# Gates of six groups projected after the scan, in two-level block products, in a Mamba2 layer with LoRA experts on one core

## The chip, the core and the metric

The kernel runs on one core of a Trainium2 chip, in fp32 throughout. The core has a matmul engine (TensorE, "PE" in the profile), three engines for elementwise work (VectorE "DVE", ScalarE "ACT", GpSimd "POOL"), and a queue for transfers ("SP"). The metric is the time of one execution on the device in microseconds.

## The reference

A block of a network with 2048 tokens of 1024 channels. The input is normalised (layer norm without weights) and goes to two branches, whose sum is added to the input.

The first branch is a Mamba2 layer. `in_proj_w` projects to gate (4096 channels), x (4096), B and C (1024 each) and dt (64 heads). There are 8 groups; a group has 512 channels of the gate, 512 of x, 128 of B and 128 of C.

```python
gate = proj[..., :I]
hbc = proj[..., I:I + CONV_DIM]
...
xBC = jax.nn.silu(conv)                  # causal, 4 taps, over hbc
...
state = state * dA_t[..., None, None] + dtx_t[..., None] * B_t[:, :, None, :]
y_t = jnp.einsum('bhpn,bhn->bhp', state, C_t)
...
y = jnp.moveaxis(ys, 0, 1) + x * D[None, None, :, None]
yn = (yg * lax.rsqrt(var + EPS)).reshape(B, L, I) * norm_weight   # var per group
yn = yn * jax.nn.silu(gate)
out = jnp.einsum('bli,di->bld', yn, out_proj_w)
```

So the gate is needed only at the end: it multiplies the normalised output of the scan just before the output projection. The second branch is a linear layer of 1024 x 1024 with bias ("base") plus a mixture of rank-16 adapters, two of eight for each token.

## The kernel before

Channels lie on the partitions and tokens along the free axis. The sequence has two halves of 1024 tokens (`s` = 0, 1), each of two blocks of 512.

**Projections.** The big products save arithmetic by Strassen's scheme (Winograd's form). `pair` takes two tiles of 128 output channels over one half of the sequence: a matrix of 2 x 2 blocks times one of 2 x 2 blocks, in 7 block products instead of 8. A product is 4 matmuls of 128 x 128 weights with 512 tokens, accumulated in a bank of PSUM (`pa`, `px`, `py` of the pool `ps_proj`, four banks). The products come in the order 1, 6, 5, 2, 7, 3, 4; the banks are pa for 1 and 2, px for 6, 7 and 4, py for 5 and 3. In between, ScalarE copies (`s1`) and VectorE adds (L478, L482, L531) take the sums out, and each finished quarter is stored to memory (`stored`). The sums of weights (`s1` to `s4`) are made by GpSimd for the first half (L427) and kept in memory for the second.

`in_pairs` sets the order of the pairs: for each half and each group, three pairs of x, B and C and two pairs of the gate (whose quarters get the SiLU and go to `gate_d`), in all 40 per half; then four pairs of the base layer for each half, the second half first. The generator `stream` walks through this order one product at a time, and loads a pair's weights one pair ahead.

**The scan.** Behind the first five pairs runs the scan. `blocks` are 32 (half, group, block), each with four chunks of 128 tokens, so there are 128 slots. A slot mixes by hand, in program order, products of the stream (`products`) with the work of one chunk: `scan_b` of this chunk (ps_y, ps_e and ps_st on TensorE, then the output, and the state's update on GpSimd and VectorE) and `scan_a` of the next (on VectorE a scan of the decays `es`, and the mask `dab`; on TensorE the product `ps_cb` and the transposes of x, `ps_xt`, both in the bank "aux"; on ScalarE `xdt` and `xdd`). Around these lie the convolution of the next block (`conv`, in the second and third slot of a block), the norm and the multiplication with the gate for the block before (`norm_gate`, first slot), the squares (`norm_squares`, last slot), in the first half the layer norm of the second half (`ln_next`, `small`), and in the second half the sums of the output weights for the two-level scheme (`out_sums`, 16 sets on GpSimd, one per block). How many products each slot gets is set by `plan`:

```python
plan = [(0, 7 * PRE), (n_slots // 2 - NQ, 7 * (5 * G + 5)), (n_slots, total)]
```

With PRE = 5, G = 8 and 88 pairs in all this makes 280 products for the first 60 slots and 287 for the other 68. The last two pairs (POST = 2, 14 products) are kept for behind the scan.

**The output stage.** The output projection runs in four passes (second half of the sequence first) in the two-level scheme: 7 outer units of 7 inner products, each product 8 matmuls with 256 tokens (banks pa, px, py again). Its weights come from the sums in memory, its operands from `y_d`, and the additions to the result are on VectorE. The 14 products that were kept run while its first loads come in.

TensorE's instructions, GpSimd's sums and some of ScalarE's are kept in program order; the others may be placed by the compiler of the tile language by what they depend on. The functions that the change touches:

## Time and profile before

| what | value |
|---|---|
| median of 3 runs | 3439.4 us (3437.9 to 3439.51) |
| the profiled execution | 3437.5 us |
| its span on the core | 3435.7 us |
| mean granted clock of TensorE | 0.998 |
| busy: TensorE / VectorE / ScalarE / GpSimd | 3404.6 / 2410.5 / 1338.9 / 697.2 us |
| moved by DMA | 769.85 MB, mean 224 GB/s |

The profile is one execution. Every matmul in fp32 is two records in it. The duration of a record includes the end of its pipeline, which overlaps the next record, so the distance from start to start is the better price. In the order of time, `x8` is a merged run of eight records, and the bracket behind a row says how long the engine had been idle and what ended that. In the groups of instructions, the columns are line, engine and operation, output and inputs with their shapes, the count, then busy time and mean duration in ns, and last the idle time of the engine before them with what ended it. A line can be that of a helper: all matmuls are L79, and the sums on GpSimd L83. Windows give the busy time of each engine in a stretch of the span, with the number of instructions in parentheses, and then the clock, the share of DMA and GB/s.

### The profile page before, as it was taken

What the parts mean: (1) busy time and instruction counts of PE and PEld (TensorE: products, weight loads), DVE (VectorE), ACT (ScalarE), POOL (GpSimd) and SP (SyncE); (2) the same over time, 40 slices, a digit from 0 to 9 for tenths busy, and PEclk for the clock granted to TensorE, in tenths of its full rate; (3) what the DMA queues carried; (4) which work ended last, traced back from release to release, by engine and by line L of the source; (5) the groups of instructions that cost most, each with busy time, mean ns of one, the idle gap of its engine ahead of it and who ended that gap; (6) DMA issues with size and microseconds to landing.
All of it is one profiled execution on the core that took longest, in us unless ns stands there. A gap on an engine that the chain in (4) does not pass through costs nothing.

```text
span 3435.7 us, 38674 instructions
## 1 busy us (share of the span) xinstructions
PE 3404.6 (99%) x12820; PEld 1989.8 (58%) x12820; DVE 2410.5 (70%) x2733; ACT 1338.9 (39%) x3694; POOL 697.2 (20%) x443
## 2 busy tenths in 40 slices
PE   9999999999999999999999999999999999999999
PEld 7444544544545544544455454454454588888888
DVE  7547776877877867777777877777875466566665
ACT  2245454554555454545545455555453000000000
POOL 4123223222222211332222332222321000000000
PEclk9999999999999999999999999999999999999999
DMA  6546655655666676887778787877777777585654
GB/s 236 190 166 198 209 184 187 216 183 196 207 196 209 196 261 219 287 261 242 235 246 256 235 255 249 254 237 240 242 237 260 256 274 242 195 300 187 214 164 144
DMA packets 530327, 769.85 MB, mean 224 GB/s; under 512 B 35152, under 2 KB 264656, under 8 KB 527440
## 3 DMA queue, kind: packets, MB, share of 16 engines
q1 hardware_dynamic: 530128, 767.39, 68.7%
q8 instruction: 102, 1.67, 0.2%
q14 instruction: 97, 0.79, 0.1%
HBM read 516.64 MB, written 250.61 MB: 223 GB/s over the span
## 4 chain that ended last, share of the span: by engine, by line
PE 87%; DVE 8%; issue 2%; DMA 2%; ACT 2%; SPq 0%; DVEq 0%; ACTq 0%
PE ps_x_x L79 12%; PE ps_x_w L79 8%; PE ps_a_x L79 8%; PE ps_y_x L79 8%; PE ps_x_g L79 8%; PE ps_y_w L79 6%; PE ps_a_w L79 6%; PE ps_y_g L79 5%; PE ps_a_g L79 5%; PE ps_y L79 3%; PE ps_e L79 3%; PE ps_st L79 3%; PE ps_x_b L79 2%; DVE xg L646 2%; PE ps_a_b L79 2%
## 5 line engine op out<-in xcount | busy, mean ns | idle before, releaser
L83 POOL TENSOR_TENSOR state<-state,tot 128x512 f32<-128x512 f32 x112 | 150.2, 1341 | 1307.6 <-PE ps_e L79 1175.7
L688 DVE TENSOR_TENSOR_SCAN es<-dab,here 128x1024 f32<-128x1024 f32 x128 | 303.5, 2371 | 82.6 <-ACT xdd L728 81.3
L646 DVE SCALAR_TENSOR_TENSOR xg<-rawx,cw,xg 128x512 f32<-128x512 f32 x384 | 338.3, 929 | 16.8 <-ACT xg L640 15.9
L79 PE MATMUL ps_x_w<-t,w 128*128 128x256 f32 x1344 | 303.8, 379 | 0.0
L720 ACT ACTIVATE xdt<-ps_xt,dt 128x64 f32<-128x64 f32 x1024 | 223.0, 331 | 203.6 <-PE ps_xt L88 203.6
L79 PEld LDWEIGHTS ps_x_w<-t,w 128*128 128x128 f32 x1344 | 255.4, 190 | 41.5 <-issue 7.7
L705 ACT ACTIVATE ps_y<-xg,dsk 128x128 f32<-128x128 f32 x512 | 190.2, 371 | 222.5 <-DVE xg L770 192.9
L1345 ACT COPY s<-ps_a_w 128x512 f32<-128x512 f32 x28 | 16.4, 585 | 636.2 <-PE ps_a_w L79 555.6
L728 ACT ACTIVATE xdd<-xdt,es 128x64 f32<-128x64 f32 x1024 | 261.7, 387 | 0.0
L83 POOL TENSOR_TENSOR wo<-wo 128x512 f32<-128x512 f32 (+1 forms) x112 | 211.9, 1892 | 6.8
L709 DVE TENSOR_TENSOR dab<-es,cbm 128x1024 f32<-128x1024 f32 x128 | 177.6, 1388 | 39.3 <-ACT cbm L698 39.0
L79 PE MATMUL ps_a_w<-q,w 128*128 128x256 f32 x896 | 202.5, 379 | 0.0
L79 PEld LDWEIGHTS ps_a_w<-q,w 128*128 128x128 f32 x896 | 170.2, 190 | 23.6 <-issue 0.5
L79 PE MATMUL ps_x_x<-op_again,s_x 128*128 128x512 f32 x384 | 172.7, 592 | 0.0
L79 PE MATMUL ps_y_x<-op_again,s_x 128*128 128x512 f32 x384 | 172.7, 592 | 0.0
L79 PE MATMUL ps_a_x<-op_again,a_x 128*128 128x512 f32 x384 | 172.7, 592 | 0.0
L79 PEld LDWEIGHTS ps_y<-dab,xdt 128*64 128x64 f32 x2048 | 112.8, 137 | 102.9 <-issue 40.8
L79 PE MATMUL ps_x_x<-op,s_x 128*128 128x512 f32 x368 | 165.5, 592 | 0.0
L79 PE MATMUL ps_y_x<-op,s_x 128*128 128x512 f32 x368 | 165.5, 592 | 0.0
L79 PE MATMUL ps_a_x<-op,a_x 128*128 128x512 f32 x368 | 165.4, 592 | 0.0
L646 DVE SCALAR_TENSOR_TENSOR bc<-rawb,cw,bc 128x512 f32<-128x512 f32 x192 | 163.8, 885 | 1.9 <-ACT bc L640 1.3
L531 DVE TENSOR_TENSOR ev<-ps_x_x,s_x 128x512 f32<-128x512 f32 x94 | 64.4, 686 | 129.3 <-PE ps_x_x L79 124.2
(238 smaller groups left out, 6152.1 us busy)
## 6 DMA issues: line engine op xcount, KB each, us to landing
w<-w SPq DMA_DIRECT2D x196, 512.0 KB, 3.7
dab<-da_d SPq DMA_DIRECT2D x128, 512.0 KB, 5.4
raw<-ev SPq DMA_DIRECT2D x192, 256.0 KB, 3.3
a_x<-in_w_in_dram SPq DMA_DIRECT2D x168, 256.0 KB, 4.0
w<-wo SPq DMA_DIRECT2D x96, 448.0 KB, 4.3
ecp<-run_d SPq DMA_DIRECT2D x256, 128.0 KB, 4.0
gate<-ev SPq DMA_DIRECT2D x128, 256.0 KB, 3.6
sg<-gate SPq DMA_DIRECT2D x32, 1024.0 KB, 7.8
```

The lines of the kernel that those rows point to most:

```text
L79: tc.keep_in_program_order(nc.tensor.matmul(*args, **kw))
L83: ins = nc.gpsimd.tensor_tensor(*args)
L531: nc.vector.tensor_tensor(e, ps, add, alu)
L646: nc.vector.scalar_tensor_tensor(dst[:, i, :], raw[:, i, k : k + TB], cw[:, ti, k : k + 1], dst[:, i, :], ALU.mult, ALU.add,)
L688: nc.vector.tensor_tensor_scan(es.rearrange("p h t -> p (h t)"), dab.rearrange("p h t -> p (h t)"), here, 0.0, ALU.mult, ALU.add,)
L705: nc.scalar.activation(psy[:, j, :], xg[:, j, cs], AF.Copy, scale=dsk[:, at : at + 1])
L709: nc.vector.tensor_tensor(ms, es, cbm.unsqueeze(1).to_broadcast([P, HG, Q]), ALU.mult)
L720: ins = nc.scalar.activation(xdt[:, h, :], x_t[:, h, :], AF.Copy, scale=dt_of[s][:, half * NQ + c, at : at + 1],)
L728: ins = nc.scalar.activation(xdd[:, h, :], xdt[:, h, :], AF.Copy, scale=es[:, h, Q - 1 : Q])
L1345: nc.scalar.copy(s1, pa)
```

## The change

The gates of groups 0 to 5 (`2 * NO`, with NO = 3) leave the stream. It then has 28 pairs per half instead of 40, and `plan` spreads these over the same 128 slots; `products` takes `min(n - 3, 1)` where a slot has only three. In `norm_gate` these groups are normalised and stored without the gate.

Behind the scan and behind the last 14 products comes a new stage of 2 halves x 3 pairs of groups (`o`) x 7 outer units. A unit is 7 inner products of 4 matmuls with 256 tokens. Its left operands come from `w_in` or, for four of the seven units, from sums `s_d`, which `oct_sums` makes on GpSimd (for the first `o` in the last block of the scan, for the others in the stage), and GpSimd makes the second level of sums in `left_two`. The right operands' second level is made on VectorE (`right_two`) once per half. The results are gathered in SBUF (`acc_g`), get the SiLU on ScalarE, are multiplied on VectorE with the normalised y, which is loaded again from `y_d`, and stored in `yg_d` (`gated`). The output stage reads these groups from `yg_d`.

Further: of the 16 sets of output-weight sums 11 stay in the scan (two blocks of three) and 5 go to the second half of the new stage. The transposes of x take the bank "st" in place of "aux"; the sums of the layer norm, `ps_tot` and `ps_sm` take "aux". The output stage goes through the first half of the sequence first. The pool of the operands (`op`) is closed after the gate stage.

```diff
+NO = 3
...
-        ps = over_channels(of, "st", f"mean_{s}_{i}")
+        ps = over_channels(of, "aux", f"mean_{s}_{i}")
...
-                for q in range(2):
+                for q in range(2 if g >= 2 * NO else 0):
                     t = 4 * g + 2 * q
                     yield pair(
...
-        pst = ps_one.tile([P, 4, Q], F32, tag="aux", name=f"ps_xt_{n}")
+        pst = ps_one.tile([P, 4, Q], F32, tag="st", name=f"ps_xt_{n}")
...
-            nc.vector.tensor_tensor(two, two, sg_of[s, g, half][:, j : j + 2, :], ALU.mult)
+            if g >= 2 * NO:
+                nc.vector.tensor_tensor(two, two, sg_of[s, g, half][:, j : j + 2, :], ALU.mult)
             nc.sync.dma_start(y_d[g][:, j : j + 2, at : at + TB], two)
...
-    plan = [(0, 7 * PRE), (n_slots // 2 - NQ, 7 * (5 * G + 5)), (n_slots, total)]
+    plan = [(0, 7 * PRE), (n_slots // 2 - NQ, 7 * (N_S + 4)), (n_slots, total)]
...
-        if 0 <= b - 15 < 16:
-            left_sums = out_sums(wo, b - 15)
+        summing = 0 <= b - 15 < 16 and (b - 15) % 3 < 2
+        if summing:
+            left_sums = out_sums(wo, n_sums)
+            n_sums += 1
...
+    order = (1, 2, 6, 5, 7, 3, 4)
+    gate_units = [(s, o, i) for s in range(NS) for o in range(NO) for i in order]
...
+    def left_two(u):
...
+        add(s1, a21, a22, ALU.add)
+        yield
+        add(s2, s1, a11, ALU.subtract)
+        yield
+        add(s4, a12, s2, ALU.subtract)
+        yield
+        add(a21, a11, a21, ALU.subtract)
+        yield
...
+    def gated(s, o, a, n, z):
+
+        at = slice(s * TS + n * TB, s * TS + (n + 1) * TB)
+        y = gy.tile([P, 2, 2, TB], F32, tag="gy", name=f"gy_{s}_{o}_{a}{n}")
+        for q in range(2):
+            nc.sync.dma_start(y[:, q], y_d[2 * o + q][:, 2 * a : 2 * a + 2, at])
+        yield
+        for q in range(2):
+            nc.scalar.activation(z[:, q], z[:, q], AF.Silu)
+            yield
+        for q in range(2):
+            nc.vector.tensor_tensor(z[:, q], z[:, q], y[:, q], ALU.mult)
+            nc.sync.dma_start(yg_d[2 * o + q][:, 2 * a : 2 * a + 2, at], z[:, q])
+            yield
...
+        if u:
+            side[0].append(lambda u=u: load_left(u + 2))
+        two = left_two(u + 1)
+        for n in range(4):
+            side[n] += steps(two, 1)
+        if o == 0 and 0 < pos < 6 or (s, o, pos) == (1, 0, 0):
+            two = right_two(s, order[pos + 1])
+            for n in (4, 4, 5, 6):
+                side[n] += steps(two, 1)
...
+        if s == 0 and o + 1 < NO and pos in (0, 2, 4, 5):
+            gen = oct_sums(gt, "wo", o + 1, (0, 2, 4, 5).index(pos))
+            side[4] += steps(gen, 1)
+            nxt[4] += steps(gen, 1)
+
+        if s == 1 and n_sums < 16:
+            if len(sum_steps) == 0:
+                gen = out_sums(gt, n_sums)
+                n_sums += 1
+                sum_steps = steps(gen, 4)
+            side[4].append(sum_steps.pop(0))
...
+        if i == 2:
+            nxt[0].append(lambda a=c11, b=k_: big_add(a, b))
+        if i == 5:
+            nxt[0].append(lambda a=c12, b=k_: big_add(a, b))
+        if i == 7:
+            nxt[0].append(lambda a=k_, b=t7: big_add(a, b))
+            nxt[1].append(lambda a=t7, b=c12: big_add(a, b))
...
+        for n, j in enumerate(inner):
+            ps = {1: pa, 2: pa, 6: px, 7: px, 4: px, 5: py, 3: py}[j]
+            for q in range(2):
+                for k in range(KQ):
+                    mm(
+                        ps[:, q, :], left[j][:, q, k, :], right[j][:, k, :],
+                        start=(n < 3 and q + k == 0), stop=(k == KQ - 1), skip_group_check=True,
+                    )
...
-    passes = [(s, p) for s in (1, 0) for p in range(2)]
+    passes = [(s, p) for s in range(NS) for p in range(2)]
...
-            nc.sync.dma_start(x, y_d[4 * p + 2 * k + h][:, :, at : at + TB])
+            g = 4 * p + 2 * k + h
+            nc.sync.dma_start(x, (yg_d if g < 2 * NO else y_d)[g][:, :, at : at + TB])
...
-    load_hw(1)
-    for _ in range(7 * POST - 5):
-        next(stream)
+    load_hw(0)
     next_ops = {}
...
+    for step in sum(nxt, []):
+        step()
+    ga_ctx.close()
+    op_ctx.close()
```

## The prediction

> **What bounds the kernel now.** I read the page's head first, then the windows by stage, then the order of time on TensorE, and last the waits. The head names the bound:
>
> ```profile
> span 3435.7 us, 38674 instructions
> PE 3404.6 (99%) x12820; PEld 1989.8 (58%) x12820; DVE 2410.5 (70%) x2733; ACT 1338.9 (39%) x3694; POOL 697.2 (20%) x443
> ```
>
> TensorE is busy for all but 31 us. A busy share alone could hide poor pipelining, so I look at starts in the order of time. One slot of the scan with four products reads:
>
> ```profile
> 1976.46 1.16 PE L79 MATMUL ps_e<-bc,state 128*128 128x128 f32 x8
> 1977.46 1.02 PE L79 MATMUL ps_st<-xdd,bt 128*128 128x512 f32 x2
> 1978.32 3.60 PE L79 MATMUL ps_x_g<-op_again,s_g 128*128 128x512 f32 x8
> 1981.75 0.39 PE L79 MATMUL ps_cb<-bc 128*128 128x128 f32 x2
> 1981.97 0.27 PE L88 MATMUL ps_cb<-ident,bc 128*128 128x128 f32 x1
> 1982.08 3.60 PE L79 MATMUL ps_y_g<-op_again,s_g 128*128 128x512 f32 x8
> 1985.52 3.60 PE L79 MATMUL ps_a_g<-op_again,a_g 128*128 128x512 f32 x8
> 1988.95 0.60 PE L88 MATMUL ps_xt<-ident,xg 128*128 128x128 f32 x4
> 1989.39 3.60 PE L79 MATMUL ps_x_g<-op_again,s_g 128*128 128x512 f32 x8
> ```
>
> Starts, not durations, give the price: a one-level product (4 fp32 matmuls of 512 columns, 8 records) takes 3.43 us; the scan's own matmuls take 3.7 us of a slot, and the mean over channels adds 0.96 us every fourth slot. Two-level products are in the output stage (from the chain of waits):
>
> ```profile
> 2726.48 3.45 PE ps_a_w L79 x16
> 2729.93 3.45 PE ps_x_w L79 x16
> 2733.38 3.45 PE ps_y_w L79 x16
> ```
>
> That is 8 matmuls of 256 columns in 3.453 us, so halving the columns costs 0.7%. Next, the stages (first half of the scan, its second half, the output stage):
>
> ```profile
> core 0: us, PE busy (x) PEld busy (x) DVE busy (x) ACT busy (x) POOL busy (x), PEclk, DMA share, GB/s
> 258.00:1290.00 1032.00, 1021.60 (x3653) 522.24 (x3652) 783.57 (x987) 538.26 (x1453) 259.52 (x168) 1.00 0.62 203
> 1548.00:2580.00 1032.00, 1024.07 (x3735) 513.94 (x3734) 776.57 (x818) 534.23 (x1528) 287.67 (x161) 1.00 0.78 244
> 2730.00:3430.00 700.00, 700.00 (x3182) 604.20 (x3181) 444.16 (x469) 18.73 (x32) 0.00 (x0) 1.00 0.66 220
> ```
>
> VectorE is 75% busy in the scan, and TensorE loses only 8 to 10 us per 1032. VectorE's own idle time there is not all slack (waits of the second half):
>
> ```profile
> L688 DVE TENSOR_TENSOR_SCAN es<-dab,here 128x1024 f32<-128x1024 f32 x56 | 129.9, 2320 | 55.6 <-ACT xdd L728 54.5 <-DMA dab<-da_d 1.1
> L709 DVE TENSOR_TENSOR dab<-es,cbm 128x1024 f32<-128x1024 f32 x56 | 79.1, 1412 | 14.9 <-ACT cbm L698 14.9
> L531 DVE TENSOR_TENSOR ev<-ps_x_x,s_x 128x512 f32<-128x512 f32 x36 | 24.7, 686 | 40.9 <-PE ps_x_x L79 40.9
> ```
>
> The first two rows are waits for ScalarE inside a slot; the third is waiting for TensorE, which is real slack.
>
> **The change, part by part.**
>
> *Arithmetic.* The gates of six groups were 2 x 6 x 2 = 24 pairs of 7 products: 168 x 3.435 = 577 us. They become 42 units of 7 products, each 4 matmuls of 256 columns: 294 x 1.7265 = 507.5 us. TensorE: -69.5 us. All of it counts, since TensorE sets the end; no other matmul is added.
>
> *The scan loses its filler.* Products between slots fall from 280 to 189 in the first 60 slots and from 287 to 210 in the last 68, so from 4.67 and 4.22 to 3.15 and 3.09 per slot. TensorE's slot becomes 3.15 x 3.43 + 3.7 + 0.24 + about 0.8 (layer norm matmuls) = 15.5 us in the first half and 3.09 x 3.43 + 3.94 = 14.5 us in the second. VectorE's work does not shrink with it. Second half: 776.6 us over 56 slots is 13.9 us per slot. A product carries 5 adds of 0.686 us per 7, so 1.13 fewer products take 0.55 off; the gate multiply (1.215 us x 64, six eighths of it, over 128 slots) takes 0.45; about 0.4 goes because VectorE's operations are stretched by GpSimd (the convolution's L646 takes 0.99 us here and 0.74 at its best) and 5 of 16 sets of output-weight sums leave. That is 12.5 us against 14.5 (86%). First half: 783.6 over 51.3 slots is 15.3, less 0.75 and 0.45, is 14.1 against 15.5 (91%). So TensorE still has more to do, but with much less room. By kind of slot the second half needs about 13 us of VectorE in the first (reciprocal 3.35, scale 3.0), 14.4 in the two with the convolution and 9 in the last, so VectorE runs late in the middle slots and catches up in the last. What is late first is an eviction: between products 7 and 4 of a pair, both in the px bank, stands one product, 3.43 us; behind it come dab for ps_y (some 5 us of room) and the state add. The bounds: zero, since in the window 860 to 946 us VectorE was 86% busy and TensorE lost nothing; and, if all of VectorE's present idle time (4.6 to 4.9 us per slot) stayed, 17.1 and 19.0 us per slot, +380 us. The nearest rows are the windows at 602, 860 and 1118 (VectorE 84 to 86% busy, TensorE loses 0 to 1.1 of 86 us), so I stay near the low end: 0.2 us per slot more than now, 26 us, and 4 us for the four layer norm pieces. +30 us.
>
> *Transposes from the aux to the st bank.* They no longer wait for ScalarE's copies of ps_cb but for the state add, which started some 3 us after ps_st's end in the traced slots, about 10 us before the transposes would start. Zero; if VectorE is 10 us late it is the next wait. Mean and variance of the layer norm go to aux: zero, one queue for another.
>
> *Gate stage, per seven units (84.6 us of TensorE).* VectorE: 47 evicting adds x 0.686 = 32, four adds of 128x2048 x 2.285 = 9.1, eight gatings x 1.215 = 9.7, together 51; in the first third of each half also 28 operand sums x 0.68 = 19, so 70. ScalarE: 15 us. GpSimd: 28 operand sums x 1.606 = 45, and either four oct sums (26) or 5/3 sets of output-weight sums of 15.7 us (26): 71. SP: at most about 62 issues of some 0.4 us = 25 us, the weight loads two units ahead; a store that waits for GpSimd blocks the y loads and the next weight loads behind it, but these lead by 24 us. DMA: 7 MB of weights, 8 MB of y in and out, 8 MB for the sums: 23 MB in 84.6 us, 272 GB/s, where the page's slices reach 300. All below 84.6, but unevenly: a unit adding into two places asks up to 13.2 us of VectorE in 12.1 (15.9 with operand sums), with only 1.73 us between products 7 and 4.
>
> Here a rule speaks against the change. In the trace GpSimd's 128x512 adds last 1.28 us at the median of the base sums and 1.606 as a mean of the output-weight sums; the longest state multiply was 3.1. The Trainium skill, "SBUF — State Buffer", section "Who interferes with whom", explains that: VectorE and GpSimd share a port pair under an exclusive lock, a tensor_tensor with both inputs in SBUF takes part, and the second to issue is blocked entirely. By the rule undisturbed GpSimd time and VectorE's two-SBUF time add up: 59 + 25 = 84 us of 84.6 in the second half, and over it by 16 to 19 us in each half's first third; up to +35 us. By the traced means it is zero beyond the local bursts. The scan ran both engines at a summed 103% with TensorE nearly undisturbed, so I take +10 us and keep 0 and 35 as ends.
>
> *Seams.* Into the gate stage: 14 base products (48 us) cover the first loads, as they covered the output stage's. Zero; without the cover, about 8 us (1 MB landed in 7.4 us). Out of it nothing covers: w and q loads are issued on SP behind the last unit's y load and yg stores, which wait for VectorE. About 4 us of the unit remain then, landing takes 3.7 and 7.4 us, and two operand sums of 1.2 us follow. 2 to 15 us; I take 7. The swapped order of halves and the moved quarter sources change no count: zero.
>
> *Sum.* -69.5 + 30 + 10 + 7 = -22.5. The profiled execution took 3437.5 us (span 3435.7), so 3415; the median of the runs, 3439.4, is 1.9 higher, so 3416 to 3417.
>
> **The rivals.**
>
> *VectorE paces the scan (slower).* One mechanism: in-order VectorE with its waits for ScalarE. Waits for xdd and cbm total about 98 us in the 56 slots, 1.75 per slot, and need not shrink. With them VectorE needs 14.3 us of 14.5 in the second half and 15.9 of 15.5 in the first. Add half of its waits for TensorE (1.4 per slot) and slots are 15.7 and 17.3: (1.2 x 68 + 1.8 x 60) = +190; a quarter, some +90. The decision is at 22.5 + 30 = 52 us, 0.41 us per slot. For it: 86 to 91% utilisation, and every traced stall on an eviction lies in a convolution slot. Against it: the 86% windows without loss. At +90 the time is 3437.5 - 69.5 + 17 + 90 = 3475.
>
> *The filler was never needed.* Scan waits stay as now and the gate stage is smooth: -69.5 + 7 + about 5, 3380.
>
> *The loss just equals the gain.* 45 to 60 us in scan and stage: 3432 to 3446, no change.
>
> *It doesn't do what it says.* The small products might not hold 1.73 us, since the operands change every 4 matmuls instead of 8. At 0.2 us a product (the issue gap seen ahead of weight loads) that is 59 us and no gain; but in the output stage 16 records follow 16 without a gap. Little weight; it lies in the slower case.
>
> **How the numbers follow.** Main case 0.44 (3398 to 3432, at 3416); filler not needed 0.15 (3375 to 3398); even 0.11; slower 0.30, mostly 3450 to 3485, with a tail to 3550. A measurement can tell 0.2%, about 7 us, from no change. Hence faster 0.59, same 0.11, slower 0.30. The range 3380 to 3480 leaves out about 0.05 below and 0.12 above; the main case alone spans 3398 to 3432.
>
> **What would show it.** Right: a gate stage of about 510 to 525 us with product starts 1.73 us apart; the scan's 128 slots in about 1960 us with VectorE at 85 to 90% there; TensorE waits on evictions (L531, L478) of a few tens of us; a gap of 5 to 10 us ahead of the first ps_a_w. Wrong: slots of 15.5 us and more with TensorE waiting for dab, ecp or state under a VectorE that is never idle (the slower rival); a gate stage above 540 us with waits for GpSimd's sums or DMA (the lock rule); or TensorE without any waits (the filler was never needed).

## The result: slower by 3.7%, and the profile after

The changed kernel takes 3563.4 us (median of 4 runs, 3560.5 to 3573.6), the kernel before 3438.7 us beside it: a ratio of 1.0368, 95% interval 1.0352 to 1.0384. The forecast was 3416 us, faster. (The profile after is that of the fastest of its four executions, 3560.5 us.) The head of the page after:

```profile
span 3558.8 us, 41191 instructions
PE 3387.2 (95%) x13828; PEld 2208.9 (62%) x13828; DVE 2628.6 (74%) x2975; ACT 1359.6 (38%) x3690; POOL 977.0 (27%) x611
```

TensorE is idle for 171.6 us instead of 31.1. And it is busy for only 17.4 us less, where 69.5 us of its work are gone. Both say that something besides the arithmetic went wrong. The windows of the kernel after, by stage: the scan up to the end of slot 63 (the last store of the first half's state), the scan's second half, the two halves of the gate stage, and 700 us of the output stage.

```profile
172.00:1232.50 1060.50, 999.04 (x3886) 531.40 (x3885) 863.47 (x1074) 631.98 (x1777) 258.56 (x168) 0.97 0.63 203
1232.50:2189.90 957.40, 930.53 (x3692) 482.91 (x3691) 795.22 (x839) 573.25 (x1691) 266.45 (x144) 1.00 0.76 241
2249.30:2533.90 284.60, 263.09 (x1177) 227.19 (x1176) 179.41 (x195) 42.22 (x56) 177.60 (x116) 0.97 0.71 241
2533.90:2846.60 312.70, 264.21 (x1177) 226.68 (x1175) 182.31 (x189) 44.84 (x59) 196.16 (x117) 0.94 0.70 224
2850.00:3550.00 700.00, 699.73 (x3177) 603.57 (x3177) 445.02 (x470) 18.79 (x32) 0.00 (x0) 1.00 0.67 228
```

The same two stretches of the scan in the kernel before:

```profile
172.00:1482.00 1310.00, 1298.61 (x4628) 659.41 (x4627) 953.32 (x1165) 669.83 (x1844) 331.73 (x216) 1.00 0.64 208
1482.00:2664.00 1182.00, 1174.07 (x4282) 589.45 (x4281) 870.40 (x917) 599.31 (x1737) 314.01 (x177) 1.00 0.78 246
```

From these I work out what each stage lost against the arithmetic. I count products by `plan` up to slot 63: 297 before (280, and 4 x 4.22), 201 after (189, and 4 x 3.09).

| stage | work removed or due | what happened | lost | forecast |
|---|---|---|---|---|
| scan, slots 0 to 63 | -95.5 products x 3.435 = -328 us | 1482.0 to 1232.5: -249.5 | 78.5 | 16 |
| scan, slots 64 to 127 | -72.5 products = -249 us | 1182.0 to 957.4: -224.6 | 24.4 | 14 |
| gate stage, less the seam | 294 x 1.7265 = 507.5 us | 583.3 us | 75.8 | 10 |
| seam out of it | 0 | 14.0 us | 14.0 | 7 |
| arithmetic | -69.5 us | | -69.5 | -69.5 |

The sum is +123.2 us, and the spans differ by 123.1 (the seam into the gate stage and the output stage moved by 3 us in opposite directions).

The granted clock stands before the DMA share in each row: 0.97 in the first half of the scan, 0.94 in the second half of the gate stage, 1.00 in the undisturbed stages. Where work was removed, TensorE's busy time should have fallen by its price. It is over that by 28 us in the scan's first half (999.0 against 1298.6 - 328), by 5 in the second, and by 20 in the gate stage (527.3 against 507.5): 53 us in which TensorE worked longer for the same matmuls. The trace keeps the granted clock as stretches at 1.00 and at 0.50. In the whole span TensorE is busy for 85.6 us at 0.50, so half of that, 43 us, is lost, against 4 us in the kernel before: 38 us of matmuls at half speed. Some 8 us more are the ends of matmuls that nothing overlaps (an estimate: 0.16 us, the 1.89 us of a product less the 1.73 from start to start, for each of 77 waits instead of 28). The few us that remain are not accounted for.

The arithmetic itself came out as forecast. Where nothing waits, products of the gate stage start 1.73 us apart:

```profile
2499.81 1.89 PE L81 MATMUL ps_a_z<-op_again,la 128*128 128x256 f32 x8
2501.53 1.89 PE L81 MATMUL ps_x_z<-op_again,la 128*128 128x256 f32 x8
2503.26 1.89 PE L81 MATMUL ps_y_z<-op_again,ls 128*128 128x256 f32 x8
2504.99 1.89 PE L81 MATMUL ps_x_z<-x,la 128*128 128x256 f32 x8
```

What TensorE waited for, over the whole span (total us, times, longest):

```profile
PE ps_y L81 <- ACT xdt L723: 35.2, 12, 6.4
PE ps_y_z L81 <- DVE s_z L1331: 21.5, 3, 12.1
PE ps_x_z L81 <- DVE s_z L1328: 19.7, 9, 7.1
PE ps_a_w L81 <- DMA w<-w: 14.2, 2, 14.0
...
PE ps_var L81 <- ACT xdd L731: 8.3, 1, 8.3
PE ps_e L81 <- ACT da L348: 8.1, 4, 3.4
```

**One slot of the scan with a layer-norm piece.** TensorE first, in order of time, then ScalarE and VectorE in the same 16 us:

```profile
734.93 1.10 PE L81 MATMUL ps_mean<-half,ones 128*128 128x256 f32 x4
...
738.84 3.60 PE L81 MATMUL ps_a_x<-op,a_x 128*128 128x512 f32 x8
...
742.60 3.60 PE L81 MATMUL ps_x_x<-op,s_x 128*128 128x512 f32 x8
746.04 0.60 PE L90 MATMUL ps_xt<-ident,xg 128*128 128x128 f32 x4
753.37 2.05 PE L81 MATMUL ps_var<-lsq,ones 128*128 128x256 f32 x4 [6.73 <-ACT xdt L723]
755.21 5.13 PE L81 MATMUL ps_y_x<-op,s_x 128*128 128x512 f32 x8
```

```profile
745.41 1.59 ACT L708 ACTIVATE ps_y<-xg,dsk 128x128 f32<-128x128 f32 x4 [8.96 <-DVE xg L773]
748.36 1.66 ACT L262 ACTIVATE lsq<-piece 128x512 f32<-128x512 f32 x3
```

```profile
749.53 0.69 DVE L264 TENSOR_TENSOR lsq<-lsq,lsq 128x512 f32<-128x512 f32 x1 [3.62 <-ACT lsq L262]
750.20 1.23 DVE L712 TENSOR_TENSOR dab<-es,cbm 128x1024 f32<-128x1024 f32 x1
...
752.54 0.68 DVE L266 TENSOR_TENSOR lsq<-lsq,lsq 128x512 f32<-128x512 f32 x1
```

The sum for the variance needs a chain: mean, subtraction on VectorE, squares on ScalarE, three additions on VectorE. The subtraction is done at 744.7, but ScalarE begins the squares at 748.36, since the output of the scan and other work stand ahead of them in its queue. The chain ends at 753.2, and `ps_var` starts at 753.37. The bracket names `xdt`; by the times it is the last addition into `lsq` that released it. TensorE had two products between the sums for mean and variance here, `ps_a_x` and the first `ps_x_x` shown. The kernel before has four in each of its four pieces, and its variance does not wait, as in the first piece:

```profile
377.55 1.03 PE L79 MATMUL ps_mean<-half,ones 128*128 128x256 f32 x4
...
392.46 3.60 PE L79 MATMUL ps_x_x<-op,s_x 128*128 128x512 f32 x8
395.89 1.03 PE L79 MATMUL ps_var<-lsq,ones 128*128 128x256 f32 x4
```

And the product behind the wait takes 5.13 us instead of 3.60.

**One stall of the gate stage.** SP, GpSimd, VectorE and TensorE in the same 38 us:

```profile
2717.71 1.46 SPq L1150 DMA_DIRECT2D la<-in_w_in_dram  x2
2735.61 0.37 SPq L902 DMA_DIRECT2D w<-wo  x1
2736.07 0.51 SPq L1226 DMA_DIRECT2D yg<-c  x1
2736.64 2.45 SPq L902 DMA_DIRECT2D w<-wo  x2
2739.18 1.32 SPq L1226 DMA_DIRECT2D yg<-c  x1
2740.55 1.23 SPq L1219 DMA_DIRECT2D gy<-y  x1
```

```profile
2728.49 7.09 POOL L85 TENSOR_TENSOR wo<-wo 128x512 f32<-128x512 f32 x4
2748.10 1.23 DVE L1225 TENSOR_TENSOR k<-k,gy 128x1024 f32<-128x1024 f32 x1 [14.39 <-DMA gy<-y]
2749.98 3.78 PE L81 MATMUL ps_y_z<-op_gate,ls 128*128 128x256 f32 x8 [12.10 <-DVE s_z L1331]
2753.55 2.65 PE L81 MATMUL ps_x_z<-x,la 128*128 128x256 f32 x8
```

SP issues nothing from 2719.2 to 2735.6: the next instruction in its queue stores a sum of output weights that GpSimd finishes at 2735.58. Behind that store wait the gate's own stores and the load of `gy`, which is issued at 2740.55. In program order it stands six products ahead of its multiplication, 10.4 us, less than the 16.4 us for which SP stood. VectorE has the multiplication with it at the head of its queue and waits 14.39 us; behind that stands the addition that frees the PSUM bank; TensorE waits 12.10 us. Then come two slow products, 3.78 and 2.65 us instead of 1.89. In the whole gate stage VectorE waits 49.7 us in five such places (`DVE k L1225 <- DMA gy<-y`), and TensorE 41.2 us for the two additions behind them.

### The profile page after: what moved, and what is told of

Its sections match the earlier page's. It is cut to its first block, busy times and chain, and to the rows that moved or that the text cites. A ratio compares the mean times of both kernels' runs of the same rounds, so it can differ in the third digit from the quotient of the medians.

```text
span 3558.8 us, 41191 instructions
## 1 busy us (share of the span) xinstructions
PE 3387.2 (95%) x13828; PEld 2208.9 (62%) x13828; DVE 2628.6 (74%) x2975; ACT 1359.6 (38%) x3690; POOL 977.0 (27%) x611
## 5 line engine op out<-in xcount | busy, mean ns | idle before, releaser
L85 POOL TENSOR_TENSOR state<-state,tot 128x512 f32<-128x512 f32 x112 | 163.5, 1459 | 1057.6 <-PE ps_e L81 935.3
L691 DVE TENSOR_TENSOR_SCAN es<-dab,here 128x1024 f32<-128x1024 f32 x128 | 316.5, 2472 | 81.4 <-ACT xdd L731 64.0
L649 DVE SCALAR_TENSOR_TENSOR xg<-rawx,cw,xg 128x512 f32<-128x512 f32 x384 | 322.1, 887 | 21.5 <-ACT xg L643 20.2
L1602 ACT COPY s<-ps_a_w 128x512 f32<-128x512 f32 x28 | 16.4, 587 | 628.3 <-PE ps_a_w L81 561.0
L85 POOL TENSOR_TENSOR wo<-wo 128x512 f32<-128x512 f32 (+1 forms) x112 | 233.8, 2087 | 14.9 <-DMA raw<-ev 7.6
L81 PEld LDWEIGHTS ps_y<-dab,xdt 128*64 128x64 f32 x2048 | 120.2, 140 | 141.3 <-ACT xdd L731 77.2
L712 DVE TENSOR_TENSOR dab<-es,cbm 128x1024 f32<-128x1024 f32 x128 | 169.5, 1324 | 49.4 <-ACT cbm L701 49.4
L81 PE MATMUL ps_y<-dab,xdt 128*64 128x128 f32 x2048 | 153.3, 288 | 43.5 <-ACT xdt L723 35.2
L429 POOL TENSOR_TENSOR s_x<-a_x,a_x 128x512 f32<-128x512 f32 x48 | 75.9, 1580 | 360.6 <-PE ps_x_x L81 119.4
```

Of the source, the lines that this page charges most:

```text
L81: tc.keep_in_program_order(nc.tensor.matmul(*args, **kw))
L85: ins = nc.gpsimd.tensor_tensor(*args)
L429: nc.gpsimd.tensor_tensor(t[what], t[x], t[y], alu)
L649: nc.vector.scalar_tensor_tensor(dst[:, i, :], raw[:, i, k : k + TB], cw[:, ti, k : k + 1], dst[:, i, :], ALU.mult, ALU.add,)
L691: nc.vector.tensor_tensor_scan(es.rearrange("p h t -> p (h t)"), dab.rearrange("p h t -> p (h t)"), here, 0.0, ALU.mult, ALU.add,)
L712: nc.vector.tensor_tensor(ms, es, cbm.unsqueeze(1).to_broadcast([P, HG, Q]), ALU.mult)
```

## The experiments

Times are medians; where a ratio is given there were four runs of the kernel against the kernel before beside it, otherwise one. "First half" and "second half" are those of the scan.

**The layer norm and the small projections behind it taken out, after and before.** The second half of the sequence takes over the first half's operands, decays and adapter weights, so the result is no longer the layer's.

```diff
-        if not (s == 0 and 0 <= i < NQ):
-            piece = after = None
+        piece = after = None
```

> The changed kernel without the layer norm and the small projections of the second half of the sequence (its operands, decays and adapter weights are those of the first half). Theory A, the chains of the layer norm between TensorE, ScalarE and VectorE no longer fit between the fewer products: the 79 us lost in slots 0 to 63 fall to under 15, and this kernel stands at most 60 us over the kernel before with the same work left out (125 with it). Theory B, VectorE's throughput paces the scan everywhere: the loss falls only in proportion to VectorE's work (91% to about 85%), and the distance stays at 90 us or more.

> The kernel before with the same work left out (layer norm and small projections of the second half of the sequence). Both theories: only the matmuls of that work go, 4 x 5.4 us for the small projections and some 10 us for means, variances and transposes, so about 3405 to 3410 us; TensorE was hardly waiting here.

3470.0 and 3392.5 us: the difference falls from 125 to 77.6. In the first half the change then saves 302.7 us (1436.8 to 1134.1) of 328, so it loses 25 instead of 78.5. So this work accounts for 53 of the 79 us, and ordinary slots for 25. Of the 53 some 39 are waiting and 15 half-speed clock (TensorE's idle time and its stretches at 0.50 in the four kernels, compared). Neither theory had its numbers: A wanted under 15 us and a distance of at most 60, B at least 90. In the kernel before the work was worth 46 us, where some 32 of its matmuls alone were expected. The second half and the gate stage do not move (963.0 and 599.3 us with the seam, against 957.4 and 597.3).

**The layer norm kept, with four products in the slots of the mean's second part and of the variance and three in the others.**

```diff
             n = target(slot) - done
+            if slot < 60:
+                n = 4 if (after, c) in ((0, 2), (1, 0)) else 3
```

> The changed kernel with the nine spare products of the first 60 slots put where the layer norm waits: four products in the third slot of each block that normalises and in the first slot of the next, three everywhere else. Same work on every engine. Theory A (latency of the chains): the waits of ps_var and of ps_y after it shrink by 3.4 us each, with their slow matmuls behind, 25 to 45 us less than 3563. Theory B (throughput of VectorE): the same work in the same time, within 10 us of 3563.

3538.5 us, ratio 1.0291 (1.0276 to 1.0307), 25 less than the change. The first half ends at 1201.3 instead of 1232.5: 31 of the 53 us come back with no operation taken away (11 of them half-speed clock that no longer follows the waits); 25 of them show in the whole time. All four pieces now have three products between mean and variance. So at least that much is the latency of the chain, not VectorE's or ScalarE's throughput.

**Does a wait slow the matmuls behind it?** In the kernel before, in its output stage, a made wait ahead of each of 27 units: a small matmul, a chain of ScalarE copies, and a second small matmul that needs its end. All of the kernel's own work stays.

```diff
+            if t + u:
+                stall(6, f"{t}_{u}")        # 26 in the longer one
```

> The kernel before with 27 made waits of TensorE of some 2 us each in the output stage (a small matmul, seven small copies on ScalarE, a small matmul that needs them, ahead of each outer unit but the first). A wait costs its own length: +50 to +65 us, and the granted clock of the stage stays at 1.00. If even short waits bring slow matmuls behind them: +100 us or more, clock under 0.97.

> The same with 27 copies, so waits of some 6 us. Theory E (a wait costs its own length): +160 to +185 us. Theory F (behind a wait of several us TensorE runs at a lower granted clock for a few us, as the records behind the longest waits of the changed kernel suggest): a further 2 to 4 us for each wait, +220 to +290 us, with the granted clock of the output stage at 0.88 to 0.94.

Two of the shorter waits, then one of the longer, in order of time on TensorE:

```profile
3019.83 0.49 PE L79 MATMUL ps_end<-pause,ident 128*128 128x128 f32 x2 [2.46 <-ACT pause L1245]
3020.15 3.62 PE L79 MATMUL ps_a_w<-q,w 128*128 128x256 f32 x16
```

```profile
2873.34 0.49 PE L79 MATMUL ps_end<-pause,ident 128*128 128x128 f32 x2 [2.46 <-ACT pause L1245]
2873.67 5.30 PE L79 MATMUL ps_a_w<-q,w 128*128 128x256 f32 x16
```

```profile
3034.32 0.79 PE L79 MATMUL ps_end<-pause,ident 128*128 128x128 f32 x2 [9.28 <-ACT pause L1245]
3034.91 6.26 PE L79 MATMUL ps_a_w<-q,w 128*128 128x256 f32 x16
3041.00 3.62 PE L79 MATMUL ps_x_w<-t,w 128*128 128x256 f32 x16
```

3542.7 and 3773.2 us, so 3.8 and 12.4 us for each wait. In all that is 103 us, as expected if even short waits bring slow matmuls (100 or more), and 334, above the 220 to 290 of theory F, as these waits lasted 9.3 us instead of 6. The mean clock granted in the stage is 0.98 and 0.87. Two waits of the same 2.46 us differ in what follows: behind one the product takes 3.62 us, its normal time, behind the other 5.30. Of the 27 short waits 12 have a slow product behind them, by 1.5 us on average. Behind all 27 long ones it is slow, by 1.1 to 2.8 us, 2.0 on average. The next product is normal in both. The granted clock around the second wait, in windows:

```profile
2871.21:2874.62 3.41, 1.28 (x7) 1.18 (x8) 3.38 (x5) 1.89 (x7) 0.00 (x0) 1.00 1.02 347
2874.62:2878.03 3.41, 3.41 (x10) 2.70 (x9) 3.41 (x2) 0.00 (x0) 0.00 (x0) 0.50 0.59 226
```

The granted clock changes at the borders of windows of 3.41 us that run through the whole trace. In the first row TensorE is busy for 1.28 of 3.41 us, 0.38 of the window, and the next window has half the clock. I counted all the windows at full clock of this case's twenty traces: each with TensorE busy for less than 0.41 of it was followed by one at 0.50, each with more than 0.49 by one at 1.00, and between these both occur. So a wait of 2.46 us costs a slow product where some 2 us of it fall into one window, and none where a border divides it more evenly. The Trainium skill, "TensorE: Matmul & The Clock Gate", section "What's actually happening", has the rule behind it: the clock is halved after an idle window of some 3.4 us and restored after a busy one. The windows and the two speeds are as it says, but the window need not be idle: here 0.38 busy was too little. The waits of the changed kernel have the same mark: 5.13 for 3.60 and 3.78 for 1.89.

**The old banks back:** the transposes of x in "aux", the sums of the layer norm, `ps_tot` and `ps_sm` in "st".

```diff
-        pst = ps_one.tile([P, 4, Q], F32, tag="st", name=f"ps_xt_{n}")
+        pst = ps_one.tile([P, 4, Q], F32, tag="aux", name=f"ps_xt_{n}")
```

> The changed kernel with the banks of before: the transposes of x in aux again, the layer norm, ps_tot and ps_sm in st. If the banks cost nothing either way: within 6 us of 3563. If the new banks are what makes the layer norm wait (aux shared with ps_cb): 20 us or more below. If they save a wait: the transposes now wait for ScalarE's copies of ps_cb with one product between, 10 to 40 us above.

3599.4 us, ratio 1.0468 (1.0453 to 1.0484): 36 us slower than the change. The largest wait of that kernel:

```profile
PE ps_xt L90 <- ACT bt L703: 54.1, 21, 6.3
```

With three products in a slot, one product stands between `ps_cb` and the transposes instead of two, and ScalarE's copies out of "aux" (L703) come late for them, as the kernel before (0.6 us in all) did not show. So the exchange of banks as a whole saves the changed kernel 36 us.

**The octant sums moved from the gate stage into the scan.** The eight sets of the second and third `o` go into two of its blocks, four to a block, and three of the five sets of output-weight sums into free blocks. No work is added or removed.

```diff
-        summing = 0 <= b - 15 < 16 and (b - 15) % 3 < 2
+        summing = 0 <= b - 15 < 16 and (b - 15) % 3 < 2 or b in (23, 26, 29)
+        oct_o = {17: 1, 20: 2, 31: 0}.get(b)
...
-        if s == 0 and o + 1 < NO and pos in (0, 2, 4, 5):
+        if False:
```

> The changed kernel with the sums of the new stage made in the scan: the eight oct sums of groups 2 to 5 in two free blocks, three of the five sets of output-weight sums in three other free blocks; two sets stay in the stage. Theory C (the transfer queue stands behind stores that wait for GpSimd, so y arrives late and VectorE waits for it in order): the 75 us lost in the stage fall to 15 to 30, the scan loses 5 to 15 more, 3510 to 3530 in all. Theory D (the stage is limited by VectorE's own bursts and the shared port): waits on s_z remain, the stage loses 50 us or more, 3550 or more.

3553.4 us, ratio 1.0336 (1.0318 to 1.0353). The gate stage falls by 56 us, to 541.1 with a seam of 13.2: it loses 20 instead of 76, as theory C expected. `DVE k L1225 <- DMA gy<-y` is gone from the waits, and TensorE's for the two additions fall from 41.2 to 2.0 us. But the second half of the scan grows by 46 us, to 1003.7, where theory C expected 5 to 15. These are single executions: those with the scan of this kernel have 998 to 1004 us, those with the scan of the change 957 to 966, so the growth is some 40 us. The halves of its gate stage:

```profile
2295.90:2556.80 260.90, 255.66 (x1177) 222.85 (x1176) 175.53 (x195) 42.13 (x56) 119.16 (x84) 1.00 0.58 199
2556.80:2837.00 280.20, 258.29 (x1177) 223.59 (x1177) 177.37 (x189) 44.75 (x59) 149.99 (x93) 0.98 0.62 203
```

Against the change's 284.6 and 298.7 less the seam these are 260.9 and 267.0: eight octant sets cost 24 us, 3.0 each, and three more sets of output weights 32 us, 10.6 each.

**The sums one to a block.** The same, but each octant set begins in a block's last slot and ends in the next block's first, over eight blocks.

```diff
+            if 15 <= b <= 22 and c == 3:
+                oct_left = oct_sums(wo, "wo", 1 + (b - 15) // 4, (b - 15) % 4)
+                next(oct_left)
```

> The octant sums of the second and third group again moved into the scan, but one set in a block, begun in the block's last slot and ended in the next block's first, over eight blocks, where the earlier kernel put four sets into each of two blocks and its scan lost 46 us more. Theory 'bursts' (four sets in one block overload that block): the scan's second half loses 10 to 20 us instead of 46, the stage stays at 541, and the time is 3510 to 3530. Theory 'a set costs 6 us wherever it lies': some 3550, like the earlier kernel's 3553.

3559.8 us, ratio 1.0354 (1.0339 to 1.037). The second half ends at 2248.9 instead of 2189.9, 59 us later (6 of them from the first half), no better than with four sets in a block. "Bursts" is refuted: the scan pays some 5 to 6 us for an octant set (40 and some 48 us over eight, the three output sets' share in it) wherever the sets lie. Its largest wait there is another than with four in a block, `PE ps_xt L90 <- DVE state L787`, 29.8 us in 8.

**Additions or transfers?** On the kernel with the sums in the scan, made work at twelve places of the gate stage's first half: additions alone, transfers alone, and both in the order of `oct_sums`.

```diff
+        yield
+        for _ in range(4):
+            add(t[:, 0], t[:, 0], t[:, 0], ALU.add)      # the first kernel
...
+        for j, src in enumerate(halves(w_in[u % 16], w_in[u % 16 + 2])):
+            nc.sync.dma_start(t[:, j], src)
+        yield
+        for j in range(4):
+            d = dram.tile([P, KH, P], F32, tag=f"mv_{u}_{j}", name=f"mv_{u}_{j}_d")
+            nc.sync.dma_start(d, t[:, j])                # the second
```

> Built on the kernel with the octant sums moved into the scan (its gate stage took 541.1 us; with eight sets of octant sums in the stage's first half it took 597.3 us). It adds made work only: at twelve places of the stage's first half four GpSimd additions of 128x512 (some 5 us), with one load of 256 KB and a store of 2 KB around them, and none of the other transfers. Theory 'additions' (GpSimd's additions, beside its own additions for the next left operand, make that operand late): the stage goes up by 35 to 85 us, to 576 to 626. Theory 'transfers' (the eight transfers of 256 KB of each set delay the queue's other loads): it goes up by less than 12 us, to under 553.

> The same kernel with the other half: at the same twelve places four loads and four stores of 256 KB each, as a set of octant sums has them, and no addition. Theory 'transfers': the stage goes up by 35 to 85 us, to 576 to 626. Theory 'additions': by less than 12 us, to under 553. If neither rises by 35 us, the cost needs both: stores that wait in the queue for the additions, with the next loads behind them.

> At the same twelve places the four loads, four additions of what was loaded, and four stores of their results, so that the stores stand in the queue behind the additions. The additions alone raised the stage by 16.2 us (541.1 to 557.3), the transfers alone by 24.2 (to 565.3). If the costs only add, the stage takes 541 + 40 = 581 us. If stores that wait for additions hold up the next loads besides, it takes 597 or more, 16 us above the sum. Under 570 the two would cover each other.

3568.2, 3567.5 and 3580.1 us. The stage takes 557.3, 565.3 and 567.8 us instead of 541.1: +16.2, +24.2 and +26.7. The first half alone (260.9 before) takes 274.5, 284.5 and 286.8. So neither of the two theories holds as it was put: both kinds of work cost, and in the stage they cover each other in great part. This rests on one execution each. In the whole time the three stand 15, 14 and 27 us higher, so there the costs would add; the scan of the second, the same code, was 8 us shorter in its one execution, while the half of the stage without made work agrees within 3 us in all of them. A set of octant sums costs 3.0 us in the real kernel and made work of both kinds 2.2, so a part of it is not reproduced. That leaves the second half, where no made work ran.

**Other rows in memory for the stores of the output-weight sums.** They write rows of 512 bytes; here the same number of stores and bytes go to rows of 3584. The output stage then reads these numbers in another order, so the result is no longer the layer's.

```diff
-            nc.sync.dma_start(w2_d[p][:, j, :, q, kt, :].rearrange("i c o -> c i o"), src)
+            flat = w2_d[p].rearrange("i j c q k o -> (i j c q k o)")
+            flat = flat.rearrange("(s c x) -> s c x", s=56, c=P)
+            nc.sync.dma_start(flat[7 * (i % 8) + j].rearrange("c (i o) -> c i o", i=7), src)
```

> The changed kernel with one thing different: the seven stores of each set of output-weight sums write 3584 bytes in a row instead of 512, as many bytes to as many stores (the output stage then multiplies by these numbers in another order, so the output is not the reference's). In the second half of the gate stage five such sets cost 298.7 us less the seam, two sets cost 267.0, so 10.6 us a set, while a set of octant sums in the first half costs 3.0. Theory 'short rows' (a store of 448 KB in rows of 512 bytes holds the queue or the DMA engines and the operands' loads behind it): the second half falls to 265 to 280 us and the time by 20 us or more, to under 3543. Theory 'additions and their order' (GpSimd's additions of 128x896 take 2.3 to 3.3 us and each store waits for one): the second half stays at 290 to 300 and the time at 3555 to 3570. The first half of the stage stays at 285 on both.

3571.3 us, ratio 1.038 (1.0363 to 1.0397), and the second half of the gate stage takes 312.9 us with a seam of 13.5, so 299.4 for 298.7. But the edit lengthens the transfers of one store in seven only. The sums of the six others lie in SBUF in runs of 512 bytes, and in the trace their packets still have 512 bytes: of 224256 such packets 14336 are gone, and 2048 of 3584 bytes have come, one store (`wox`) of each of the 16 sets. In this stage that store landed after 8.1 us at the median in both kernels. So short rows are excluded for this store, and untested for the others. What is left for the 32 us is the additions, the order in the queue, as in the stall shown above, and the transfers.

**The order in the queue alone.** First the load of y issued four products sooner; then every store of a sum issued some products behind the addition that makes it (with two octant sets and no output set moved to the scan).

```diff
-            side[5] += steps(end, 1)
+            side[1] += steps(end, 1)         # the first kernel
```

```diff
+        level_one_sums(t)
+        yield
+        store(0, t[:, :, 0])                 # the second: each group of stores a step later
```

> The changed kernel with one edit in the new stage: the loads of y for the gating are issued after the first product that follows the quarter instead of after the fifth (side[1] for side[5]), ahead of the same unit's sums on the queue. Theory C (VectorE waits in order for y, which stands behind stores that wait for GpSimd): y lands up to 7 us earlier, of the 75 us lost in the stage 30 to 45 remain, 3525 to 3545 in all. Theory D (VectorE's own bursts and the shared port): no change, 3555 to 3570.

> The changed kernel with the stores of the stage's sums issued some seven products later than the additions they wait for (side[1] of the next unit for side[4]), so that the transfer queue does not stand behind GpSimd; two of the eight oct sums move to a free block of the scan. GpSimd's work in the stage is nearly the same. Theory C (it is the queue that stands): the stage loses 20 to 35 us where it lost 75, 3515 to 3535 in all. Theory C2 (GpSimd's amount of work limits the stage): the waits for its sums stay, the stage still loses 60 or more, 3550 to 3565.

3554.2 us, ratio 1.0337 (1.032 to 1.0354), and 3554.6, ratio 1.0333 (1.0317 to 1.0348). The stage less its seam falls from 583.3 to 569.1 and 565.8. VectorE's waits for `gy` fall from 49.7 to 27.8 and 27.1 us, TensorE's for the additions behind them from 41.2 to 19.6 and 14.7. The seam grows meanwhile, from 14.0 to 16.1 and 19.5, so the time falls by only 9 us. Theory C expected more of both (3525 to 3545 and 3515 to 3535); the second lies in the range of C2, by which GpSimd's amount of work is the limit. So the order accounts for 14 us of the 76 in the first kernel and for at most 18 in the second, some 6 of which are the price of the two octant sets that it moved. Half of the `gy` waits are left in place.

**The seam's loads on ScalarE's queue.**

```diff
-                    nc.sync.dma_start(w, w2_d[p][slot, j - 1])
+                    (nc.sync if len(seam_w) >= 6 else nc.scalar).dma_start(w, w2_d[p][slot, j - 1])
```

> The changed kernel with the first six weight loads and the first quarter of the output stage issued by ScalarE's queue instead of SP's. If the 14 us at the seam are SP's order (loads behind the last stores of the gating): 5 to 10 us less, 3553 to 3558. If they are landing time or the place in memory: unchanged, 3560 to 3566.

3576.9 us, ratio 1.0398 (1.0383 to 1.0414), no gain. The wait at the seam shrinks from 14.0 to 8.9 us, while the loads' issue alone takes 12.3 us on ScalarE's queue (3.9 on SP's), and the output stage is 7.5 us longer. Why that stage grew was not settled.

**Together.** Late stores, early y, the seam on ScalarE's queue, and the layer norm's slots; then the same with NO = 2 (four groups); then the spread sums, the early y and the layer norm's slots.

> Four edits together: products steered to the layer norm, deferred stores, y loaded earlier, the seam's loads on ScalarE's queue. If the losses are separate they add: -25, -45, -5, -7, about 3480; still above the kernel before, since slots of three products lose some 0.4 us each (50 us) and the rest of the layer norm some 25.

> The same four edits with the gates of four groups moved instead of six (NO = 2; one more set of output-weight sums in the scan), four products in every slot of the blocks with the layer norm and its small projections. The gain in arithmetic falls to 46 us. If a slot of three products is what loses and one of four loses nothing: scan 15 to 25, stage 10, seam 7, so 3425 to 3435. If the loss goes with the vector work and not with the count of products: 3455 or more.

> The spread sums, the layer-norm pieces placed behind four products as in the earlier kernel that did this (31 us in the first half of the scan), and the load of y issued four products sooner. If the three causes are separate, the gains add: under 'bursts' some 3480 to 3500, otherwise 3515 to 3525. On either theory it stays slower than the kernel before (3439), since what the stage and the ordinary slots of the scan lose isn't touched.

3521.6 us, ratio 1.0237 (1.0222 to 1.0253); 3507.2, 1.0197 (1.018 to 1.0214); 3526.0, 1.0258 (1.0241 to 1.0275). The first misses what was expected (3480) by 42 us; the second lies in the upper case (3455 or more). With late stores and early y together the gate stage less its seam is 563.5 us, 20 less than the change, where 50 was expected: the two gains overlap. The last is what adding gives: 3559.8, less 25 for the layer norm, less 9 for the early y, is 3525.8. So these two causes are separate; the time lies a microsecond above the upper of the two ranges set for it, as the spread sums gained nothing. With four groups, and four products in the slots of the layer norm, the variance no longer waits, yet the first half loses 44 of the 227 us removed (its largest wait is that of `ps_y` for `xdt`, 21 us in five places), the second 6, and the gate stage less its seam of 18.3 takes 40 us more than the 338 of its products. No version comes near 3439.

## Why the prediction was wrong

**Arithmetic, -69.5 us: right.** Small products start 1.73 us apart. The rival "small products might not hold 1.73 us" is out.

**The scan's loss of its filler, +30: mis-sized, 103 us in the runs.** Two terms failed. The four layer-norm pieces were put at 4 us, as matmuls only; with the small projections behind them they cost 53, since with three products in a slot TensorE reaches the variance before the chain through VectorE and ScalarE ends. The 0.2 us a slot for the rest was read from windows with VectorE 84 to 86% busy, which had four or five products to hide each wait; measured, the ordinary slots cost about 25 us in each half, 0.4 a slot, twice as much. VectorE at 81 and 83% busy is no more loaded than in those windows. What changed was the length of cover, not the load: with less to run between a result and its use, TensorE met the latency of chains that had been hidden. For 31 us of the layer norm's loss this is shown, for the ordinary slots it is inferred from their waits. The rival "VectorE paces the scan" had the loss (90 us) nearly right and named in-order VectorE with its waits for ScalarE as the mechanism. That was luck in part, since it spread the loss over all slots, where half of it came from four pieces of layer norm. And for these it is a chain of latencies and not throughput, since one more product in two slots of each piece recovered 31 us.

**Transposes in the other bank, zero: nearly right for the new bank**, where they wait 5.4 us in four places, for the state add that I had named as the next wait. But I had not asked what the old bank would cost in the new slots: 36 us more.

**Gate stage, +10 with 35 as the end: mis-sized, 75.8.** The step that failed is the sentence that a store waiting for GpSimd blocks the y loads and the next weight loads, "but these lead by 24 us". The weight loads do, two units ahead; a y load stands only six products ahead of its use in program order, 10.4 us. In the stall shown it stood behind a store that held SP for 16.4 us and behind the gate's own stores; it landed 14.4 us late, in VectorE's queue ahead of the additions that free the banks. Without most of the sums the stage lost 20 us. Of the 56 us that the sums cost, some 24 lie with the octant sets, and made additions, made transfers and both give 14, 24 and 26 us there for half as many sets again; some 32 lie with three sets of output weights. The queue's order explains 14 of the 76, and 20 with the late stores and two octant sets moved. How the rest divides between GpSimd's additions, the transfers with their rows and the order was not separated and stays open, and whether the port lock that I weighed plays a part in it no run here shows: in twelve sets of made additions GpSimd's mean for 128x512 was 1.51 us, between the median of 1.28 and the mean of 1.606 that I had compared.

**The seam out, 7 us: right in mechanism, 14.0 measured**, of which issue and landing were the sum that I had put at 2 to 15:

```profile
2829.16 4.59 SPq L1226 DMA_DIRECT2D yg<-c  x2
2833.80 2.10 SPq L1390 DMA_DIRECT2D q<-yg  x2
2835.95 3.93 SPq L1361 DMA_DIRECT2D w<-w  x6
```

The first load of `w` is issued behind the stores of `c`, at 2835.95, and TensorE starts at 2846.64. The seam into the gate stage cost nothing, as forecast.

**Left out: matmuls at half speed behind waits, 38 us.** No term of the sum had them, since the mean clock of the kernel before is 0.998. They are not a separate cause but a surcharge on waits, and they are contained in the losses above.

## What to carry to other kernels

Filler that another engine's chain hides behind has two prices: its time, and the cover it gives. Before thinning it, list for each chain between two instructions of the bounding engine how long it takes and how much work stands between them, for the rarest slot too; busy shares do not show this. And a store that waits for a slow engine should not stand in a queue ahead of a load that an in-order engine needs. Waits of TensorE cost more than they last: one of 9.3 us cost 2.0 us more on average here, and one of 2.5 us 1.5 more in 12 of 27 cases.

## What the hardware showed

A wait of TensorE of 9.28 us made the product behind it slower in 27 cases of 27, one of 2.46 us in 12 of 27. The granted clock went to 0.50 for the next 3.41 us when TensorE had been busy for less than 0.41 of a window of that length. Made transfers like those of the octant sums, 96 of 256 KB in some 280 us, made that half of the stage 24 us longer at a DMA share of 0.79, while the second half of the scan runs at 0.76 with TensorE 97% busy. Additions on GpSimd and the transfers beside them did not add up in the stage: 14 and 24 us alone, 26 together, in one execution each.
